# An AdaLN block with a routed feed-forward on one core: last parts of 128 or 64 tokens, and a first chunk in two halves

## The chip, the cores and the metric

The kernel runs on one core of one Trainium2 chip. The metric is the device time of one execution in microseconds (us). The core has a matrix engine (TensorE, PE in the profile), a vector engine (VectorE, DVE), a scalar engine (ScalarE, ACT), a general engine (GpSimd, POOL), a sync engine that issues transfers (SP), and 16 DMA engines. All data are fp32. One fp32 matmul appears in the trace as two records.

## The reference

`x` has 4 sequences of 1024 tokens with 256 features. Six rows of modulation per sequence come from `c`. Then there is a gated linear recurrence and a feed-forward in which each token goes to 2 of 8 experts.

```python
mod = (silu(c) @ wmod).reshape(4, 6, 1, 256)
sa, ca, ga, sb, cb, gb = mod[:, 0], ..., mod[:, 5]      # ga, gb: magnitude at least 0.25
h = layernorm(x) * (1 + ca) + sa
x = x + ga * attn(h)
h = layernorm(x) * (1 + cb) + sb
x = x + gb * ffn(h)

def attn(x):
    xn = rms_scale * x / (rms(x) + EPS) * split_scale
    K = sigmoid(xn @ W_K)
    u, g_in, g_out = split(xn @ W_ugg, 3)
    u = u * sigmoid(g_in) * (1 - K)
    s = scan(s_t = K_(t-1) * s_(t-1) + u_t)
    return (s * sigmoid(g_out)) @ W_out + x

def ffn(x):
    weights, experts = normalised top 2 of softmax(x @ Wg + bg)
    return sum over the two e of weight * (gelu(x @ W1[e] + b1[e]) @ W2[e] + b2[e])
```

## The kernel before

The order of the work on all five engines is the order in which the program writes it (`manual_schedule`). Each engine runs its own list in that order, and semaphores make it wait for the others.

The first part goes through the 4096 tokens in eight chunks of 512 (`c_` from 0). A chunk is normalised and modulated, scaled by its root mean square, turned so that features lie on partitions (`hT`), and multiplied by the four projections `k`, `gi`, `u`, `go`: in `project`, four columns blocks `hc` of 128, each four products of 512 tokens. VectorE does the scan, TensorE the product with `W_out`. In the same loop the gate product `pl` (`f_gate`, L564) runs in four groups of 32 PSUM partitions, and the tokens are entered in one list for each expert.

The first chunk has its own code, since nothing has been prepared for it. It loads `c`, `x` and the modulation matrix `wmod`; `keep_busy(n)` issues n transposes whose result nobody reads; `pt_c` is the transposed silu(c), from which `scT` and `scB` are copied; `pm` (L991) is the modulation of the first sequence on all partitions, and `all_rows` (L290) that of all four. VectorE computes the statistics (a power on POOL between), ScalarE the normalisation, then come the two modulation steps per tile (L996, L999), the squares, the root, and the scale. Eight transposes `pta` (L1014) and two copies (L1015, L1016) make `hT`, and `project(0, 0)` starts with `pk` (L417). `other_rows` and the statistics of chunk 1 follow on VectorE.

The second part goes through the experts' lists in blocks of 256 tokens (`TK`). There can be up to 39 blocks (`NJ`). With two experts for each of 4096 tokens there are at least 32 (`sure`). Which expert a block `j` belongs to and where it starts in the list is computed on the chip: three tables, the last in `late_table`, which is written when block 8 is at work. A block consists of:

- `fetch_used`: the entries of block j+3, and, with two blocks' lead, a gather of the rows `hb` by POOL and the expert's weights by SP;
- `b_up`: the first product `ph` (256 to 1024 features) on the rows turned earlier (`xT`), with gelu on ScalarE;
- `b_turn(j + 1)`: VectorE turns the rows of the next block (L915);
- `b_down`: the second product `pye` (1024 to 256 features, L958) in two parts `t` of 128 tokens; each has its bias added (L972), is multiplied by its weight and gate (L973), and is added to the output by an indirect DMA from POOL (`add_rows`, L945).

The last block of an expert is filled only in part. If it has no more than 128 tokens it is a half block: 128 columns in the first product, one part in the second. In `late_table`, whole blocks and half blocks are counted; all whole ones come first in the order. The number of whole ones (`n_whole`) and of all (`n_blocks`) is loaded into registers, and from block 28 on a branch chooses the code for a whole or a half block (`work_either`). From block 32 on, each further block lies in the branch of the one before (`rest`).

Scatters into the output must not overtake each other, as two blocks can hold the same token. From block 31 on the last part of a block is therefore kept in `last_y`, with its places in `last_at` (L968 copies them), and the scatter is issued at the start of the next block:

```python
def rest(j: int):
    with tc.If(n_blocks > j):
        add_rows(last_y, last_at, T)
        work_either(j, True)
        if j + 1 < NJ:
            rest(j + 1)
```

There is one `last_y`, so it can only be written again when the scatter that reads it has landed.

Of the kernel before, what the change touches and what calls it, by code (L numbers as in the profile page):

```python
# [19 lines left out]
def tile_adaln_block(  # L20
# [33 lines left out]
    nc = tc.nc  # L54
# [92 lines left out]

    nc.sync.dma_start(out=c_sb, in_=c)
    load_x(0, nc.scalar)
    nc.sync.dma_start(out=wmod_sb[:, :, : 2 * D], in_=wmod_r[:, :, : 2 * D])  # L150
    nc.sync.dma_start(out=wmod_sb[:, :, 2 * D :], in_=wmod_r[:, :, 2 * D :])
# [5 lines left out]
    load_x(2, nc.sync)  # L157


    nc.gpsimd.memset(wg_sb, 0.0)  # L160
# [52 lines left out]
    def stats(xb, what: str):  # L213

        st = small.tile([P, TPB, 6], F32, tag="st", name=f"st_{what}")
        mv = small.tile([P, TPB, 2], F32, tag="mv", name=f"mv_{what}", bufs=4)
        rstd = small.tile([P, TPB], F32, tag="rstd", name=f"rstd_{what}", bufs=4)
        for n in range(TPB):
            nc.vector.bn_stats(st[:, n, :], xb[:, n, :])
        for n in range(TPB):  # L220
            nc.vector.bn_aggr(mv[:, n, :], st[:, n, :])
        nc.vector.tensor_scalar_add(rstd, mv[:, :, 1], LN_EPS)  # L222
        nc.gpsimd.tensor_tensor(rstd, rstd, expo[:, 0, :], ALU.pow)  # L223
        return mv, rstd

    def shift(c_):
        mv, rstd = X[c_]["stats"]
        nmr = small.tile([P, TPB], F32, tag="nmr", name=f"nmr_{c_}")
        X[c_]["nmr"] = nmr
        nc.vector.scalar_tensor_tensor(nmr, mv[:, :, 0], -1.0, rstd, ALU.mult, ALU.mult)  # L230

    def norm(dst, c_):
        xb, nmr, (_, rstd) = X[c_]["x"], X[c_]["nmr"], X[c_]["stats"]
        for n in range(TPB):
# [25 lines left out]
    def keep_busy(n: int):  # L260

        for _ in range(n):
            nc.tensor.transpose(idle[:, :P], ident, ident)  # L263

    keep_busy(14)
# [3 lines left out]
    nc.vector.tensor_copy(scT.rearrange("p k b -> p (k b)"), pt[:, : KC * B])  # L269

    scB = setup.tile([P, KC, P], F32, tag="scB", name="scB")
    nc.vector.tensor_copy(scB, scT[:, :, 0:1].broadcast_to((P, KC, P)))
    keep_busy(8)
    mda = deep.tile([P, 2, D], F32, tag="mda", name="mda_0")
# [3 lines left out]
    nc.scalar.dma_start(out=b1_sb, in_=b1.rearrange("e (c p) -> (e c) p", p=P))  # L278
    nc.scalar.dma_start(out=wg_sb[:, :, :E], in_=Wg.rearrange("(k p) e -> p k e", p=P))
    nc.scalar.dma_start(out=bg_sb, in_=bg.rearrange("(o e) -> o e", o=1).broadcast_to((P, E)))  # L280
    X[0]["stats"] = stats(X[0]["x"], "a0")
    shift(0)
    a_norm(0)

    rows_sb = setup.tile([B, 6, D], F32, tag="rows_sb", name="rows_sb")

    def all_rows(i: int):
# [9 lines left out]
        nc.scalar.copy(rows_sb[:, 2 * i : 2 * i + 2, :].rearrange("b r d -> b (r d)"), pm[:B, :])  # L297
# [66 lines left out]
    def a_square(c_):  # L364
        u = work.tile([P, TPB, D], F32, tag="u", name=f"u_{c_}", bufs=1)
        X[c_]["u"] = u
        h = X[c_]["h"]
        ss = small.tile([P, TPB], F32, tag="ss", name=f"ss_{c_}")
        X[c_]["ss"] = ss
        for n in range(TPB):  # L370
# [4 lines left out]
    def a_root(c_):  # L375
        ss = X[c_]["ss"]
        nc.vector.tensor_scalar(ss, ss, 1.0 / D, 1e-30, ALU.mult, ALU.max)
        nc.gpsimd.tensor_tensor(ss, ss, expo[:, 1, :], ALU.pow)

    def a_scale(c_):  # L380
        h, ss, u = X[c_]["h"], X[c_]["ss"], X[c_]["u"]
        nc.vector.tensor_scalar_add(ss, ss, RMS_EPS)
        nc.vector.reciprocal(ss, ss)
        for n in range(TPB):
# [17 lines left out]
    def project(c_, hc, mid=()):  # L402
# [11 lines left out]
        def product(w, col, what):  # L414
            ps = ps_mm.tile([P, TB], F32, tag="mm", name=f"p{what}_{c_}_{hc}")
            for k in range(KC):
                nc.tensor.matmul(  # L417
                    ps,
                    lhsT=w[:, k, col : col + P],
                    rhs=hT[:, k, :],  # L420
# [5 lines left out]
        ps = product(wk_sb, hc * P, "k")  # L426
# [818 lines left out]
```

## Time and profile before

| | |
|---|---|
| median of three runs | 787.91 us (787.7 to 790.15) |
| the profiled execution | 789.1 us |
| its span, first to last instruction | 787.4 us |
| mean granted TensorE clock | 0.997 |
| TensorE busy | 772.8 us, 98% |
| VectorE busy | 504.3 us, 64% |
| GpSimd busy | 290.3 us, 37% |
| ScalarE busy | 241.7 us, 31% |

All times in the profile come from one execution and count from the start of its span. In a line of a timeline the columns are: start, duration, engine, line of the code, operation, tile written and tiles read, shape, count of instructions, and in brackets how long the engine idled before it and what ended that. A line with `x16` stands for sixteen instructions in a row. In the table of stretches each engine's column is its busy time in the stretch and the number of instructions, followed by the granted clock, the busy share of the DMA engines, and GB/s. The chain of waits follows the work back from the last instruction and gives each engine's share of the span.

### The profile page before, as it was taken

What the parts mean: (1) busy time and instruction counts of PE and PEld (TensorE: products, weight loads), DVE (VectorE), ACT (ScalarE), POOL (GpSimd) and SP (SyncE); (2) the same over time, 40 slices, a digit from 0 to 9 for tenths busy, and PEclk for the clock granted to TensorE, in tenths of its full rate; (3) what the DMA queues carried; (4) which work ended last, traced back from release to release, by engine and by line L of the source; (5) the groups of instructions that cost most, each with busy time, mean ns of one, the idle gap of its engine ahead of it and who ended that gap; (6) DMA issues with size and microseconds to landing.
All of it is one profiled execution on the core that took longest, in us unless ns stands there. A gap on an engine that the chain in (4) does not pass through costs nothing.

```text
span 787.4 us, 10804 instructions
## 1 busy us (share of the span) xinstructions
PE 772.8 (98%) x3279; PEld 577.1 (73%) x3279; DVE 504.3 (64%) x1391; ACT 241.7 (31%) x560; POOL 290.3 (37%) x370
## 2 busy tenths in 40 slices
PE   8999999999999999999999999999999999999995
PEld 5455545454546557888888888888888888888994
DVE  5787877898789869767547453544536354453563
ACT  4434243534433343223222122221312222131231
POOL 2102010106142712456564564634434243343431
PEclk9999999999999999999999999999999999999998
DMA  8321334042313265799469898898878687885781
GB/s 296 95 70 47 116 102 142 23 127 86 100 55 113 55 185 183 241 328 258 73 161 206 249 247 253 245 294 223 235 211 230 186 235 217 218 232 167 221 264 25
DMA packets 116040, 138.13 MB, mean 175 GB/s; under 512 B 25782, under 2 KB 100090, under 8 KB 115968
## 3 DMA queue, kind: packets, MB, share of 16 engines
q1 hardware_dynamic: 97184, 111.46, 45.0%
q0 software_dynamic: 17216, 25.25, 15.9%
q10 hardware_dynamic: 1568, 0.57, 0.3%
q8 instruction: 32, 0.52, 0.3%
q14 instruction: 40, 0.33, 0.1%
HBM read 113.52 MB, written 25.42 MB: 176 GB/s over the span
## 4 chain that ended last, share of the span: by engine, by line
PE 83%; DMA 8%; DVE 4%; issue 2%; POOL 1%; ACT 1%; POOLq 0%; DVEq 0%
PE ph_False L928 25%; PE pye_False L958 23%; PE pya L454 7%; PE pk L417 6%; PE pgi L417 6%; PE pu L417 6%; PE pgo L417 6%; DMA hb<-hx,ent 5%; DMA out_dram<-yb_False,ent 2%; PE idle L263 1%; DMA proj<-in_L_ffn_W_dram 1%; PE pm L290 1%; PE pta L399 1%; PE pl L564 1%; DVE s L443 0%
## 5 line engine op out<-in xcount | busy, mean ns | idle before, releaser
L937 ACT ACTIVATE g_False<-ph_False,bb 128x256 f32<-128x256 f32 x248 | 103.8, 470 | 303.0 <-issue 188.2
L915 DVE STREAM_TRANSPOSE xT<-hb 32x128 f32<-32x128 f32 (+1 forms) x576 | 168.8, 293 | 12.7 <-DMA hb<-hx,ent 3.6
L958 PE MATMUL pye_False<-w,g_False 128*128 128x256 f32 x672 | 148.7, 379 | 0.0
L928 PE MATMUL ph_False<-xT,w 128*128 128x256 f32 x672 | 148.6, 379 | 0.0
L928 PEld LDWEIGHTS ph_False<-xT,w 128*128 128x128 f32 x672 | 127.4, 190 | 17.9 <-issue 0.7
L958 PEld LDWEIGHTS pye_False<-w,g_False 128*128 128x128 f32 x672 | 127.5, 190 | 17.6 <-issue 0.2
L945 POOL DMA_INDIRECT out_dram<-yb_False,ent x46 | 73.4, 1595 | 139.9 <-DVE yb_False L973 138.4
L972 DVE TENSOR_TENSOR yb_False<-pye_False,b2b 128x256 f32<-128x256 f32 x42 | 17.8, 424 | 126.3 <-PE pye_False L958 123.8
L586 POOL DMA_INDIRECT lists<-pay,placei x64 | 66.4, 1037 | 38.5 <-DMA ent<-lists 27.4
L928 PE MATMUL ph_False<-xT,proj 128*128 128x256 f32 x320 | 70.8, 379 | 0.7 <-DMA proj<-in_L_ffn_W_dram 0.7
L958 PE MATMUL pye_False<-proj,g_False 128*128 128x256 f32 x320 | 70.7, 379 | 0.0
L928 PEld LDWEIGHTS ph_False<-xT,proj 128*128 128x128 f32 x320 | 60.7, 190 | 9.3 <-DVE yb_False L972 1.0
L958 PEld LDWEIGHTS pye_False<-proj,g_False 128*128 128x128 f32 x320 | 60.8, 190 | 8.3
L830 POOL DMA_INDIRECT hb<-hx,ent x53 | 55.6, 1048 | 22.4 <-issue 15.6
L417 PE MATMUL pk<-hT,proj 128*128 128x512 f32 x128 | 61.0, 599 | 0.7 <-ACT hT L1015 0.7
L223 POOL TENSOR_TENSOR rstd_f<-rstd_f,expo 128x4 f32<-128x4 f32 x8 | 8.2, 1022 | 142.4 <-DVE rstd_f L222 98.8
L417 PE MATMUL pu<-hT,proj 128*128 128x512 f32 x128 | 60.2, 592 | 0.0
L417 PE MATMUL pgo<-hT,proj 128*128 128x512 f32 x128 | 60.2, 592 | 0.0
L417 PE MATMUL pgi<-hT,proj 128*128 128x512 f32 x128 | 60.2, 592 | 0.0
L454 PE MATMUL pya<-wo,z 128*128 128x256 f32 x256 | 56.8, 380 | 0.0
L454 PEld LDWEIGHTS pya<-wo,z 128*128 128x128 f32 x256 | 48.4, 190 | 8.6 <-issue 2.4
L972 DVE TENSOR_TENSOR yb_False<-pye_False,wo_sb 128x256 f32<-128x256 f32 x20 | 8.5, 424 | 60.4 <-PE pye_False L958 60.3
(234 smaller groups left out, 811.1 us busy)
## 6 DMA issues: line engine op xcount, KB each, us to landing
w<-in_L_ffn_W_dram SPq DMA_DIRECT2D x48, 1024.0 KB
proj<-in_L_ffn_W_dram SPq DMA_DIRECT2D x24, 1024.0 KB
hx<-gb SPq DMA_DIRECT2D x4, 1024.0 KB
out_dram<-x SPq DMA_DIRECT2D x8, 512.0 KB
hx<-h SPq DMA_DIRECT2D x8, 512.0 KB
x<-in_L_attn_x_dram SPq DMA_DIRECT2D x7, 512.0 KB
swapped<-u SPq DMA_DIRECT2D x7, 512.0 KB
hT<-swapped SPq DMA_DIRECT2D x28, 128.0 KB
```

What stands on the lines that cost most here:

```text
L223: nc.gpsimd.tensor_tensor(rstd, rstd, expo[:, 0, :], ALU.pow)
L263: nc.tensor.transpose(idle[:, :P], ident, ident)
L417: nc.tensor.matmul(ps, lhsT=w[:, k, col : col + P], rhs=hT[:, k, :], start=(k == 0), stop=(k == KC - 1),)
L454: nc.tensor.matmul(py[:, t, :], lhsT=z[hc][:, ts(2 * q + t, P)], rhs=wo[:, hc, :], start=(hc == 0), stop=(hc == HC - 1),)
L586: ins = nc.gpsimd.indirect_dma_start(out=lists[:, :], out_offset=IndirectOffsetOnAxis(ap=place, axis=0), in_=what, in_offset=None, bounds_ ...
L830: nc.gpsimd.indirect_dma_start(out=hb[:, t, :], out_offset=None, in_=hx[: seen(j), :], in_offset=IndirectOffsetOnAxis(ap=BK[j]["ent"][:, t ...
L915: nc.vector.transpose(to[ts(q, SQ), :, :, ts(i, SQ)], hb[ts(i, SQ), :, :, ts(q, SQ)])
L928: nc.tensor.matmul(ph[:, u, :], lhsT=w1[:, k, ts(fc, P)], rhs=xT[:, k, :n], start=(k == 0), stop=(k == KC - 1),)
L937: nc.scalar.activation(g[:, fc, :n], ph[:, u, :], AF.Gelu_apprx_tanh, bias=bb[:, fc : fc + 1])
L945: return nc.gpsimd.indirect_dma_start(out=out_rows[:n], out_offset=IndirectOffsetOnAxis(ap=at, axis=0), in_=yb, in_offset=None, bounds_che ...
L958: nc.tensor.matmul(py, lhsT=g[:, fc, ts(t, P)], rhs=w2[:, fc, :], start=(fc == 0), stop=(fc == FC - 1),)
L972: nc.vector.tensor_add(yb, py, b2b)
```

## The change

In the second part, a block can now have 256, 192, 128 or 64 tokens (`sizes`). The first product has 256 columns for the first two and 128 for the last two, as before. The last part of the second product has 128 or 64 tokens, chosen by a branch that stands around this part alone. A part of 64 tokens writes its eight products alternately to partitions 0 to 63 and 64 to 127 of the PSUM tile, and VectorE adds both halves. `late_table` counts four kinds of blocks, so its tables have 32 columns instead of 16, and four numbers are loaded into registers instead of two. Branches begin at block 26 instead of 28.

In the first chunk, `x` is loaded in two halves of 256 tokens on two queues; statistics, normalisation, squares, root, scale, turn, and the four products of `hc` 0 are done by halves. The loads of `b1`, `Wg` and `bg` move from ScalarE's queue to SP's, behind the `x` of chunk 2. `keep_busy` issues fp32 matmuls on zeros instead of transposes, 12 and 5 of them instead of 14, 8 and 18. The copies of `scT` and `scB` move from VectorE to ScalarE, and those of the `all_rows` results go behind the scale of the second half. `first_turn(1)`, `other_rows` and the statistics of chunk 1 come between the products of the two halves.

```diff
...
     nc.sync.dma_start(out=c_sb, in_=c)
-    load_x(0, nc.scalar)
+    nc.scalar.dma_start(out=X[0]["x"][:, halves[0]], in_=x0[:, halves[0]])
     nc.sync.dma_start(out=wmod_sb[:, :, : 2 * D], in_=wmod_r[:, :, : 2 * D])
+    nc.sync.dma_start(out=X[0]["x"][:, halves[1]], in_=x0[:, halves[1]])
...
     load_x(2, nc.sync)
+    nc.sync.dma_start(out=b1_sb, in_=b1.rearrange("e (c p) -> (e c) p", p=P))
     nc.gpsimd.memset(wg_sb, 0.0)
+    nc.sync.dma_start(out=wg_sb[:, :, :E], in_=Wg.rearrange("(k p) e -> p k e", p=P))
+    nc.sync.dma_start(out=bg_sb, in_=bg.rearrange("(o e) -> o e", o=1).broadcast_to((P, E)))
...
         for _ in range(n):
-            nc.tensor.transpose(idle[:, :P], ident, ident)
-
-    keep_busy(14)
+            nc.tensor.matmul(idle[:, :P], lhsT=zero, rhs=zero, start=True, stop=True)
+
+    keep_busy(12)
...
-    nc.vector.tensor_copy(scB, scT[:, :, 0:1].broadcast_to((P, KC, P)))
-    keep_busy(8)
...
+    nc.scalar.copy(scB, scT[:, :, 0:1].broadcast_to((P, KC, P)))
+    keep_busy(5)
...
+    for at in halves:
+        stats_of(X[0]["x"], tiles0, at)
+        shift(0, at)
+        norm(X[0]["h"], 0, at)
...
+            half, done = TB // 2, {}
+            for what in args:
+                if what == "go":
+                    halved()
+                done[what] = product(*args[what], what, slice(0, half))
+
+            def out_of(what):
+                return product(*args[what], what, slice(half, TB), done[what])
...
+    QT = P // 2
+    sizes = [TK, TK - QT, P, QT]
+    NS = len(sizes)
...
-        whole = blocks_of(float(P - 1), "lw")
-        some = blocks_of(float(TK - 1), "ls")
...
+        upto = [
+            blocks_of(float(TK - 1 - (sizes[k + 1] if k + 1 < NS else 0)), f"l{k}")
+            for k in range(NS)
+        ]
...
+    def down_part(j: int, t: int, n: int = P, mid=None, keep: bool = False):
+
+        g, w2, b2b, ent, hb = (BK[j][k] for k in ("g", "w2", "b2b", "ent", "hb"))
+        py = ps_y.tile([P, D], F32, tag="y", name=f"pye_{j}_{t}_{n}")
+
+        beside = P // n
+        for fc in range(FC):
+            nc.tensor.matmul(
+                py[ts(fc % beside, n), :],
+                lhsT=g[:, fc, ds(t * P, n)],
+                rhs=w2[:, fc, :],
+                start=(fc < beside),
+                stop=(fc >= FC - beside),
+            )
...
+        nc.vector.tensor_add(yb[:n], py[:n], b2b[:n])
+        if beside > 1:
+            nc.vector.tensor_add(yb[:n], yb[:n], py[n:])
...
-    for n in range(TPB):
+
+    def first_mod(n: int):
...
+    for n in range(HT):
+        first_mod(n)
+    a_square(0, halves[0])
+    a_root(0, halves[0])
     nc.vector.tensor_mul(rs_sb, rms_sb, split_sb)
-    for i in range(6 * D // TB):
+    first_mod(HT)
+    a_scale(0, halves[0])
+    for n in range(HT + 1, TPB):
+        first_mod(n)
+    a_square(0, halves[1])
+    for i in range(6 * D // TB - 1):
         all_rows(i)
-    keep_busy(18)
-    a_scale(0)
...
+    first_turn(0)
+    all_rows(6 * D // TB - 1)
+    a_root(0, halves[1])
+    nc.scalar.copy(mda[:, 0, :], pm[:, :D])
+    nc.vector.tensor_scalar_add(mda[:, 1, :], pm[:, D:], 1.0)
+    a_scale(0, halves[1])
+    all_rows_copied()
...
+        project(
+            c_, 0, [lambda: a_norm(nxt)] if more else [],
+            None if c_ else lambda: (
+                first_turn(1), other_rows(), load_mdf(0), a_stats(1), shift(1)
+            ),
+        )
...
+        def large():
+            first(False)
+            down_part(j, 0)
+            either(
+                j, 0, lambda: down_part(j, 1, keep=keep), lambda: down_part(j, 1, QT, keep=keep)
+            )
+
+        def small_():
+            first(True)
+            either(
+                j, 2, lambda: down_part(j, 0, keep=keep), lambda: down_part(j, 0, QT, keep=keep)
+            )
+
+        either(j, 1, large, small_)
...
```

`first` issues `fetch_used`, `b_up` and `b_turn(j + 1)`. `either(j, k, larger, smaller)` builds only `larger` where block j must, on any routing, be among the first kinds up to k, only `smaller` where it cannot be, and otherwise both in a branch on the register `n_upto[k]`.

## The prediction

> **What bounds the kernel now.** I read the page first, then the busy time by stretches, then the timelines of the last 45 us and of the first 25 us, because the diff touches only these two ends and one table in the middle. The page:
>
> ```profile
> span 787.4 us, 10804 instructions
> PE 772.8 (98%) x3279; PEld 577.1 (73%) x3279; DVE 504.3 (64%) x1391; ACT 241.7 (31%) x560; POOL 290.3 (37%) x370
> PE 83%; DMA 8%; DVE 4%; issue 2%; POOL 1%; ACT 1%; POOLq 0%; DVEq 0%
> ```
>
> TensorE is busy 98% of the span, so a saving must take matmul time away or fill the 14.6 us in which it idles. The stretches tell where (columns: length, then busy time and count of each engine):
>
> ```profile
> 429.00:700.00 271.00, 271.00 (x1258) 238.51 (x1257) 131.24 (x408) 65.40 (x156) 118.22 (x122) 1.00 0.83 235
> 742.00:778.00 36.00, 35.60 (x242) 32.85 (x240) 24.46 (x96) 11.40 (x40) 11.12 (x8) 1.00 0.71 206
> ```
>
> In the whole blocks nothing but TensorE counts. In the tail its idle time is also small (0.4 us), but the timelines show that a second chain runs just beside it:
>
> ```profile
> 735.16 7.07 PE L958 MATMUL pye_False<-w,g_False 128*128 128x256 f32 x32
> 742.07 3.73 PE L928 MATMUL ph_True<-xT,w 128*128 128x128 f32 x32
> 763.30 3.81 PE L928 MATMUL ph_True<-xT,w 128*128 128x128 f32 x32
> 770.41 3.73 PE L928 MATMUL ph_True<-xT,proj 128*128 128x128 f32 x32
> 773.98 3.62 PE L958 MATMUL pye_True<-proj,g_True 128*128 128x256 f32 x16
> ```
>
> ```profile
> 759.21 4.00 DVE L915 STREAM_TRANSPOSE xT<-hb 32x64 f32<-32x64 f32 x16 [1.00 <-DMA hb<-hx,ent]
> 764.55 0.15 DVE L968 COPY last_at<-ent 128x1 int32<-128x1 int32 x1 [1.35 <-DMA out_dram<-last_y,last_at]
> 765.64 4.00 DVE L915 STREAM_TRANSPOSE xT<-hb 32x64 f32<-32x64 f32 x16
> 770.16 0.15 DVE L968 COPY last_at<-ent 128x1 int32<-128x1 int32 x1 [0.52 <-DMA out_dram<-last_y,last_at]
> 777.63 0.42 DVE L972 TENSOR_TENSOR last_y<-pye_True,wo_sb 128x256 f32<-128x256 f32 x1 [1.82 <-PE pye_True L958]
> ```
>
> ```profile
> 771.83 1.56 POOL L945 DMA_INDIRECT out_dram<-last_y,last_at  x1 [4.37 <-DVE last_y L973]
> 778.93 1.56 POOL L945 DMA_INDIRECT out_dram<-last_y,last_at  x1 [5.55 <-DVEq L1203]
> ```
>
> The reader should see that L968 waits for the previous scatter to land before `last_y` may be overwritten, that VectorE turns the next block's rows for 4.0 us, and that block 34's first product (763.30) starts when its turn ends (763.21), not when TensorE is free.
>
> **The tail.** From the router on these inputs the experts get 1849, 1836, 484, 383, 1127, 837, 1258 and 418 tokens. Cut in 256s, the remainders are 57, 44, 228, 127, 103, 69, 234 and 162. Before, that is 31 whole and 5 half blocks, as the trace has it. After, 30 whole, one of 192 (j=30), three of 128 (31 to 33) and two of 64 (34, 35). The first product is not changed. A second-product part is 16 records of 0.216 us, 3.45 us. The part of 64 tokens has the same 16 records, put alternately in the two halves of PSUM's partitions; it is shorter only if two of them run side by side. The nearest row is the gate product, which uses four groups of 32 columns:
>
> ```profile
> 95.88 0.65 PE L564 MATMUL pl<-hT,wg_sb 128*32 128x128 f32 x16
> ```
>
> Sixteen records of 128 columns at 0.108 us (half of the 256-column 0.216) would take 1.73 us one after another; they took 0.65. So groups do overlap, here 2.7-fold for four. [...]
>
> [...] Each 64-token part has one more VectorE add (0.42 us, the row of L972, because the halves are summed). I carry the timeline forward, each step with its own duration of before:
> - Block 30: the second part ends at 740.35 instead of 742.07; three VectorE steps (0.42+0.42+0.48) instead of two; the scatter goes out at 742.25 instead of 743.50.
> - Block 31: b_up from 740.35, down to 747.4; its scatter 749.45 (750.73 before). Its landing took 6.4 us, so L968 goes at 755.85 (757.15), scatter 32 at 757.15, and lands 6.1 us later (as before) at 763.25.
> - hb(34) is gathered 1.9 us behind that scatter, at 751.3, lands 6.5 us later at 757.8, is turned by 761.9: b_up(34) at 761.95 instead of 763.30. Its 64-token down ends at 767.4.
> - Block 35: VectorE first waits for that landing, does block 33's steps (1.1), then turns 4.0 to 768.35: b_up(35) at 768.4 instead of 770.41, although TensorE was free at 767.4. Down ends at 773.9 instead of 777.6.
> - Block 34's `last_y` comes after that turn: scatter 770.7 instead of 771.83; it lands 3.8 us later at 774.5; block 35's four steps (0.15+0.42+0.42+0.48) and the 0.58 to issue give the last scatter at 776.55 instead of 778.93.
>
> So 2.4 us of the 5.2 arrive at the end. Bounds: -1.0 if the gather of 34 lands no earlier (the 16 DMA engines are full with weights from 752 to 769), -3.5 if landings are as short as the shortest, 3.7 us. The weights of 35 landed at 768.9 and are needed at 772.1, so they cover. What lies behind the last scatter (8.4 us: landing and the closing barrier) is kept.
>
> Branches: 10 blocks (j from 26) instead of 8 are branched, each with a second branch between its two products, and four registers are loaded instead of two (0.3 to 0.5 us each at 697). On TensorE a compare-and-branch took 0.07 to 0.22 us, twice more (0.445 at 738.46, 3.70 at 775.37), and it is fetched 2 to 3 us ahead of the array, so I cost them at nothing. VectorE has about 0.5 us at each, hidden in its waits for scatters (0.5 to 2.7 us idle). Price without that cover: 0.2 us for each of 10 on TensorE, 2 us. [...] I use the ordinary rows, because before's five half blocks already jump over a whole variant and only one jump was long.
>
> **The table.** `late_table` runs 429.59 to 435.05 on VectorE. Two more `blocks_of` (0.6 each), two more differences and starts (0.6), and four operations on 736 instead of 368 elements (0.54 to about 0.93, 1.56 in all), two more folds (0.8): +4.2 us. Behind it wait block 8's `yb` steps, its scatters on POOL and the gather of block 11. Their next need is at 452 to 453, and VectorE idles half of that stretch (131 of 271 us), so I cost it at nothing; if block 11's rows come late, up to 4 us.
>
> **The front.**
>
> ```profile
> 4.69 0.37 PE L268 MATMUL pt_c<-ident,sc 4*128 4x4 f32 x2
> 6.75 2.25 PE L991 MATMUL pm<-wmod_sb,scB 128*128 128x512 f32 x4
> 14.18 2.19 PE L263 MATMUL idle<-ident 128*128 128x128 f32 x18
> 17.91 1.98 PE L417 MATMUL pk<-hT,proj 128*128 128x512 f32 x4 [0.67 <-ACT hT L1015]
> ```
>
> TensorE waits here for VectorE and ScalarE. The keep-busy products become true fp32 ones, two records each: 24 records ahead of pt_c instead of 14. At 0.21 us each (the cold row: 14 took 3.25) that is 5.1 us from about 1.05, and pt_c slips from 4.69 to 6.2, with the scT and scB copies, pm and the first `first_mod` behind it: pm ready at 10.0 instead of 9.0. [...] Against this, x arrives in halves, so statistics, mods, root and scale of half 0 are done before half 1's; the four products of half 0 start (256 columns, 0.86 us each) while half 1 is finished. I get pk at 16.65 instead of 17.91, and project(0,0) done at 24.0 instead of 25.05. The small loads moved from ScalarE's queue pass to SP's, behind x2 and ahead of x3: three issues of about 0.5 us there, not needed before 90 us. The 18 fillers go; the gaps of 1.5 to 2 us that they leave lie after 8 us of dense matmuls. Then `other_rows` and the statistics of chunk 1 come some 2.5 us later on VectorE, so nu·pu and go wait and hold PSUM buffers: about 0.4 us of TensorE waits come back. Net -0.9 us; bounds -2.0 (warm early) and +0.5 (cold, with a longer VectorE line).
>
> Sum: -2.4 + 0 + 0 - 0.9 = -3.3 us. The profiled execution took 789.1 (span 787.4), so it would be 785.8 (784.1). That one stands 1.2 above the median of the runs, 787.91; from the median, 784.6.
>
> **The rivals.**
> - *The whole TensorE saving arrives*: scatters land faster than in the trace, the tail gives 5.2 and the front 0.9: 781.8. For it: TensorE has 98%. Against: the rows of L968 and of xT above.
> - *The two ends give nothing*: the column halves do not overlap, or the chain alone sets the tail, and the front's slip of pt_c eats its gain: 787.5 to 788. Here the change doesn't do what it says. For it: 24 cold records ahead of pt_c. Against: the pl row.
> - *Slower: code fetch at the branches*. Ten blocks get a jump between the two products where before there was straight code. If such a jump stalls for the 3.7 us of the long record, less the 2 us lead, five or more misses of 1.7 us cost 8.5 against 3.3: 793. It decides from the second miss (2 x 1.7 = 3.4) on. For it: the 0.445 and the 3.70. Against: all ordinary jumps.
>
> **How the numbers follow.** Likeliest case (chain-limited tail, small front gain) 50%, 783.0 to 786.4; whole saving 17%; nothing 16%; slower 17%. About 0.3% (2.4 us) is what a measurement of this kernel can tell from no change, so faster means below 785.5. The likeliest case lies below that by four fifths: 0.40 + 0.17, with a little from the nothing case, 0.58 faster; 0.25 same; 0.17 slower. The range reaches from 781.5 to 789.5.
>
> **What would show it.** Right: second parts of j = 30, 34 and 35 in 1.7 to 1.8 us; block 35's first product about 2 us after block 34's last matmul has ended or less, waiting for xT; the last scatter 2 to 3 us nearer. Front: pk at 16 to 17. Wrong: 64-token parts of 3.4 us; TensorE idle with only branches ahead of it; pk later than 17.9; idle TensorE near 452 to 460; a lower granted clock in the first slices.

## The result, and the profile after

The changed kernel takes 795.34 us in the median of six runs (794.11 to 801.89), the kernel before beside it 788.41 (787.7 to 790.46). The ratio is 1.0098, with a 95% interval of 1.0077 to 1.0118: 6 to 9 us slower, where 3.3 us faster was forecast. The profiled execution took 795.39 us (span 793.7).

The same three lines of the page as the prediction shows, now of the changed kernel (called "after" from here on):

```profile
span 793.7 us, 11029 instructions
PE 769.4 (97%) x3289; PEld 573.7 (72%) x3289; DVE 509.6 (64%) x1412; ACT 242.4 (31%) x563; POOL 290.4 (37%) x373
PE 43%; DMA 27%; issue 14%; POOL 7%; DVE 5%; ACT 1%; POOLq 1%; another core or an unknown queue 0%; SPq 0%; DVEq 0%
```

TensorE's busy time fell by 3.4 us on balance, and the timeline below shows the shorter parts. But it idles 24.3 us of the span instead of 14.6, and its share of the chain that ended last went from 83% to 43%. The waits of TensorE in after (columns: who waited for what, us in total, times, longest) name the new ones:

```profile
PE ph_False L996 <- DMA w<-in_L_ffn_W_dram: 3.2, 1, 3.2
PE ph_True L996 <- DVE yb L1044: 1.9, 1, 1.9
PE ph_True L996 <- DVE xT L983: 1.7, 1, 1.7
PE ph_True L996 <- issue: 1.5, 1, 1.5
PE ph_False L996 <- DVE yb L1041: 1.1, 2, 0.6
```

All five stand ahead of a block's first product (L996). TensorE's timeline of after places them:

```profile
455.06 7.14 PE L996 MATMUL ph_False<-xT,w 128*128 128x256 f32 x32 [3.25 <-DMA w<-in_L_ffn_W_dram]
...
718.33 7.17 PE L996 MATMUL ph_False<-xT,proj 128*128 128x256 f32 x32 [0.57 <-DVE yb L1041]
...
732.98 7.17 PE L996 MATMUL ph_False<-xT,w 128*128 128x256 f32 x32 [0.57 <-DVE yb L1041]
739.99 5.49 PE L1028 MATMUL pye<-w,g 128*128 128x256 f32 x32
747.42 3.81 PE L996 MATMUL ph_True<-xT,w 128*128 128x128 f32 x32 [1.93 <-DVE yb L1044]
...
770.45 3.81 PE L996 MATMUL ph_True<-xT,w 128*128 128x128 f32 x32 [1.55 <-issue]
774.19 2.01 PE L1028 MATMUL pye<-w,g 128*64 128x256 f32 x16
777.87 3.84 PE L996 MATMUL ph_True<-xT,proj 128*128 128x128 f32 x32 [1.67 <-DVE xT L983]
781.64 2.01 PE L1028 MATMUL pye<-proj,g 128*64 128x256 f32 x16
```

The reader sees the shorter parts (7.07 became 5.49, 3.62 became 2.01) and, around them, idle stretches that add up to more than they saved. Start times in both executions, and what lies between:

| | before | after | difference |
|---|---|---|---|
| `project(0, 1)` starts | 24.89 | 24.19 | -0.70 |
| block 9, first product | 438.18 | 437.84 | -0.34 |
| block 12 (past the late weights of block 10) | 479.62 | 482.76 | +3.14 |
| block 30 (past two waits of 0.57) | 728.26 | 732.98 | +4.72 |
| block 31 (one part of 64, then 1.93 idle) | 742.07 | 747.42 | +5.35 |
| block 33 | 756.12 | 761.55 | +5.43 |
| block 34 (turn of rows late) | 763.30 | 770.45 | +7.15 |
| block 35 (part of 64, turn late) | 770.41 | 777.87 | +7.46 |
| last scatter | 778.93 | 785.43 | +6.50 |

Ahead of block 34 the profile names no cause ("issue"), but VectorE's turn of its rows ends at 770.36, 0.09 us before the product:

```profile
766.36 4.00 DVE L983 STREAM_TRANSPOSE xT<-hb 32x64 f32<-32x64 f32 x16 [0.72 <-DMA hb<-hx,ent]
```

The table is of one execution of each kernel. It leaves four questions: the late weights of block 10, behind the longer `late_table` (+3.5), the waits of 0.57 (+1.6), the stall ahead of block 31 (2.2 from start to start, after a part that saved 1.7), and the tail.

### The profile page after: what moved, and what is told of

The parts are those of the page before. It is cut to its first block, busy times and chain, and to the rows that moved or that the text cites. A ratio compares the mean times of both kernels' runs of the same rounds, so it can differ in the third digit from the quotient of the medians.

```text
span 793.7 us, 11029 instructions
## 1 busy us (share of the span) xinstructions
PE 769.4 (97%) x3289; PEld 573.7 (72%) x3289; DVE 509.6 (64%) x1412; ACT 242.4 (31%) x563; POOL 290.4 (37%) x373
## 4 chain that ended last, share of the span: by engine, by line
PE 43%; DMA 27%; issue 14%; POOL 7%; DVE 5%; ACT 1%; POOLq 1%; another core or an unknown queue 0%; SPq 0%; DVEq 0%
DMA out_dram<-yb,ent 13%; DMA hb<-hx,ent 8%; PE pya L505 7%; PE pk L449 6%; PE pgi L449 6%; PE pgo L449 6%; PE pu L449 6%; PE ph_False L996 5%; POOL out_dram L1014 5%; PE pye L1028 4%; DMA lists<-pay,placei 4%; DMA ent<-lists 3%; PE idle L286 1%; POOL lists L638 1%; PE pta L430 1%
## 5 line engine op out<-in xcount | busy, mean ns | idle before, releaser
L1005 ACT ACTIVATE g<-ph_False,bb 128x256 f32<-128x256 f32 x248 | 104.0, 471 | 308.0 <-issue 158.2
L1028 PE MATMUL pye<-w,g 128*128 128x256 f32 (+1 forms) x720 | 156.5, 380 | 0.4 <-DMA w<-in_L_ffn_W_dram 0.4
L996 PE MATMUL ph_False<-xT,w 128*128 128x256 f32 x672 | 148.8, 380 | 3.8 <-DMA w<-in_L_ffn_W_dram 3.2
L1028 PEld LDWEIGHTS pye<-w,g 128*128 128x128 f32 (+1 forms) x720 | 132.6, 188 | 20.1 <-issue 1.5
L996 PEld LDWEIGHTS ph_False<-xT,w 128*128 128x128 f32 x672 | 127.3, 190 | 22.4 <-issue 4.3
L1014 POOL DMA_INDIRECT out_dram<-yb,ent x46 | 73.2, 1592 | 146.6 <-DVE yb L1044 145.0
L1028 PE MATMUL pye<-proj,g 128*128 128x256 f32 (+1 forms) x352 | 76.3, 379 | 0.0
L1028 PEld LDWEIGHTS pye<-proj,g 128*128 128x128 f32 (+1 forms) x352 | 64.9, 188 | 9.1
L996 PE MATMUL ph_False<-xT,proj 128*128 128x256 f32 x320 | 70.9, 380 | 0.6 <-DVE yb L1041 0.6
L996 PEld LDWEIGHTS ph_False<-xT,proj 128*128 128x128 f32 x320 | 60.6, 190 | 9.3 <-DVE yb L1041 1.0
L449 PE MATMUL pk<-hT,proj 128*128 128x512 f32 (+1 forms) x132 | 61.2, 585 | 0.2 <-ACT rows_sb L327 0.2
L449 PE MATMUL pgo<-hT,proj 128*128 128x512 f32 (+1 forms) x132 | 60.4, 580 | 0.0
L449 PE MATMUL pu<-hT,proj 128*128 128x512 f32 (+1 forms) x132 | 60.3, 579 | 0.0
L449 PE MATMUL pgi<-hT,proj 128*128 128x512 f32 (+1 forms) x132 | 60.3, 579 | 0.0
```

The costliest lines, as they stand in the source:

```text
L449: nc.tensor.matmul(ps[:, at], lhsT=w[:, k, col : col + P], rhs=hT[:, k, at], start=(k == 0), stop=(k == KC - 1),)
L996: nc.tensor.matmul(ph[:, u, :], lhsT=w1[:, k, ts(fc, P)], rhs=xT[:, k, :n], start=(k == 0), stop=(k == KC - 1),)
L1005: nc.scalar.activation(g[:, fc, :n], ph[:, u, :], AF.Gelu_apprx_tanh, bias=bb[:, fc : fc + 1])
L1014: return nc.gpsimd.indirect_dma_start(out=out_rows[:n], out_offset=IndirectOffsetOnAxis(ap=at, axis=0), in_=yb, in_offset=None, bounds_che ...
L1028: nc.tensor.matmul(py[ts(fc % beside, n), :], lhsT=g[:, fc, ds(t * P, n)], rhs=w2[:, fc, :], start=(fc < beside), stop=(fc >= FC - beside),)
```

## The experiments

Ratios are to runs of the kernel before on the same chip, with 95% intervals; 0.1% is 0.8 us. Where two kernels are compared by their ratios and ran on different chips, the text gives both figures or a range. A trace is one execution, and what it shows need not be in the others. In the diffs, lines with + are new.

**The first chunk alone.** e1 is before with the hunks of the first chunk and none of the blocks.

> The kernel before with the first-chunk part of the change alone; blocks, table and branches as before. Theory: this part gives what the trace of after shows at block 8 and no more, TensorE 0.34 us earlier at 438 us, so 0.3 to 0.7 us faster than before, and the 6.5 us that after lost are all in the other part. Rival: part of the loss comes from the front (chunk 1's statistics later, small loads later), then this kernel is 1 us or more slower than before.

Measured: 1.0012 (1.0002 to 1.0023), about 1 us slower. At block 8 TensorE waits for weights in its trace, for 2.19 us where the trace of before has 0.67:

```profile
425.97 8.83 PE L980 MATMUL ph_False<-xT,proj 128*128 128x256 f32 x32 [2.19 <-DMA proj<-in_L_ffn_W_dram]
```

The 32 records took 8.83 us instead of 7.07. The stretches of the same kernel show why (the figure after the engines is the granted clock):

```profile
428.00:430.00 2.00, 2.00 (x6) 1.55 (x5) 1.87 (x8) 0.84 (x2) 1.69 (x2) 0.50 1.12 72
```

After 2.19 us of idle the clock stood at half for some 3.5 us (the two stretches around this one, 426 to 428 and 430 to 432, have 0.70 and 0.95). The stall cost its 2.19 us and 1.76 more. That is more than the kernel loses in its median: the traced execution took 793.0 us, the median of 14 is 790.58. So the place is shown, the usual size is not.

**A slower table in before.** e2:

```diff
             tab["l"], ends_at = late_table()
+            spare = wo_sb.rearrange("p c d -> p (c d)")[:, D:]
+            for _ in range(4):
+                nc.vector.tensor_add(spare, spare, spare)
+            nc.vector.tensor_add(spare[:, :D], spare[:, :D], spare[:, :D])
```

> The kernel before with five idle additions (4.3 us of VectorE, results unused) right behind late_table in block 8; nothing else. Theory: the longer table alone makes block 10's weights late, through block 8's scatters, the list scatter behind them on GpSimd, and the load of a block's entries that stands ahead of the weights on SP's queue; TensorE idles about 3 us ahead of block 10's first product, and the kernel is 3 us slower than before. Rival: the idle time at 455 us in after comes from other traffic, and VectorE's slack hides 4 us here as I had forecast: no idle time, same as before within 0.5 us.

Measured: 1.0043 (1.0025 to 1.0061), 2 to 5 us slower, by nothing but VectorE work that I had called hidden. Its trace has the wait in the same place, block 10's first product; before's trace, shown first, has none there:

```profile
451.99 7.07 PE L928 MATMUL ph_False<-xT,w 128*128 128x256 f32 x32
```

```profile
452.80 7.14 PE L928 MATMUL ph_False<-xT,w 128*128 128x256 f32 x32 [1.65 <-DMA w<-in_L_ffn_W_dram]
```

The way is seen on the queues of GpSimd (first line) and SP. Before:

```profile
438.17 1.03 POOL L586 DMA_INDIRECT lists<-pay,placei  x1 [0.19 <-issue]
443.10 0.37 SPq L822 DMA_DIRECT2D ent<-lists  x1
444.15 0.25 SPq L852 DMA_DIRECT2D w<-in_L_ffn_W_dram  x1
```

After:

```profile
442.50 1.03 POOL L638 DMA_INDIRECT lists<-pay,placei  x1 [0.19 <-issue]
445.83 0.37 SPq L890 DMA_DIRECT2D ent<-lists  x1
446.76 0.37 SPq L920 DMA_DIRECT2D w<-in_L_ffn_W_dram  x1
```

Block 10's weights were issued 7.84 us ahead of their use in before (452.0). In after they were used 8.30 us after their issue, as soon as they were there, so before can have had little room to spare. They are issued 2.61 us later in after, because the load of a block's entries stands ahead of them on SP's queue. That load waits for a list scatter on POOL (4.33 us later), and this stands behind block 8's scatter into the output (440.59 instead of 436.26), which waits for VectorE, which is at the table.

**The table in block 11.** e3 is after with the table moved:

```diff
-        elif j == NE:
+        elif j == NE + 3:
             tab["l"], ends_at = late_table()
```

> The kernel after with late_table written in block 11 instead of block 8 (it is needed from block 14 on); its size is unchanged. Theory: from block 10 on the weights are fetched a block earlier, so the cover is there, the 3.25 us of idle TensorE ahead of block 10 vanish, and the kernel is 3.0 to 3.3 us faster than after. Rival: another wait of a block's weights takes its place in block 13 or 14, and it gains under 1 us.

The wait for block 10's weights is gone from the trace. The time is 1.0070 (1.0045 to 1.0095), against 1.0098 and, in a second measurement (e5), 1.0078 for after. So only 0.6 to 2.2 us reach the end, where 3.0 to 3.3 were expected, and the intervals overlap: no gain is shown. In the traced execution what was won was partly lost later: 2.48 us idle ahead of block 31 (1.93 in after), and 3.18 us ahead of block 35 (1.67), followed by a clock of 0.50.

**The small variant first.** e4 is after with the two variants of a block exchanged in the code:

```diff
+            if k == 1:
+                with tc.If(n_upto[k] < j + 1) as it_is:
+                    smaller()
+                with it_is.Else():
+                    larger()
+                return
```

> The kernel after with the two variants of a block exchanged in the code: the one with 128 columns in the first product stands ahead of the one with 256. Theory: TensorE's 2.97 us compare-and-branch at 743.9 is a fetch of code, because the jump from the end of block 30's large variant over its small one and block 31's large one is the longest in the kernel; with the order exchanged no jump there is that long, the record falls under 0.5 us, block 31's first product starts 2 us earlier, and the kernel is 1 to 2 us faster than after. Rival 1: TensorE waited there for VectorE (the profile names yb L1044), which stays, so no change. Rival 2: the miss moves to another block, for instance at the first large block or the end, and costs as much.

Measured: 1.0036 (1.0021 to 1.0051), 3 to 5 us less than after, more than expected. TensorE's compare-and-branch instructions in before, after and e4 (columns: engine queue, count, shortest/median/longest in ns, first and last start):

```profile
L1153 PEldq COMPARE_BRANCH  x11: 65/185/445, 697.8 to 768.5; - x11
```

```profile
L1252 PEldq COMPARE_BRANCH  x25: 65/179/2967, 684.2 to 779.6; - x25
```

```profile
L1258 PEldq COMPARE_BRANCH  x18: 65/178/331, 685.5 to 777.6; - x18
```

The record of 2967 ns in after starts at 743.91 and ends 0.5 us before block 31's first product. The page had put this wait down to `yb`; e4 leaves VectorE's work as it is, and block 31 starts without idle time. The way there passes block 30's small variant and block 31's large one, 72 matmuls of code; in before the same way passed 56, and its branch took 445 ns. With the small variant first nothing that long is passed.

What the branch waited for is seen on the DMA queue q8, which the page calls an instruction queue. In the whole blocks of before and after it carries one packet of 16 KB for each 255 or so instructions of TensorE, matmuls and weight loads almost all of them (237 to 272 between two packets), so it brings TensorE's code. Between 743.9 and 746.9 it has one packet (columns: packets, MB, share of 16 engines), from 744.57 to 745.53:

```profile
q8 instruction: 1, 0.02, 2.0%
```

The four other records of 3.2 to 3.5 us (e3, e5, e13b, e14b) have one each, begun 0.7 us after the record's start and ended 1.1 to 1.4 us before its end. Ahead of block 10, where the weights were late, there is none. So I take the wait ahead of block 31 for a fetch of code. The record took 3.0 to 3.5 us in these five traces, of which 1.9 to 2.6 us showed as idle time in four.

What e4 won is more than this stall's 2 us, and the rest was not isolated. Its trace also has 0.37 us instead of 1.55 ahead of block 34, and the exchange moves all code behind it.

**The changed kernel again**, beside the next three:

> The changed kernel itself, beside the next three on one chip. Theory: 6 to 8 us slower than before, as in the first comparison; the trace shows again the late weights of block 10, two waits of about 0.57 us ahead of the first products of blocks 29 and 30, and one compare-and-branch of about 3 us ahead of block 31. Rival: one or more of these were chance of one execution, then they are missing here and the time is 2 us or more nearer to before.

Measured: 1.0078 (1.0051 to 1.0105). All waits are there again, but their sizes differ: block 10 waited 0.61 us in this execution, block 31 2.30 and then ran at a clock of 0.50 (5.31 us instead of 3.73), block 35 3.04 and again at half clock (5.47). It is the slowest of six (798.4 us, median 796.62). The kinds of waits are the kernel's, their sizes are one execution's.

**Three repairs together**: e6 is after with the late table, the small variant first, and at the end of each small variant

```diff
+            for _ in range(2):
+                nc.vector.memset(spare, 0.0)
```

> The kernel after with late_table in block 11, the small variant ahead of the large one in the code, and two one-column memsets on VectorE at the end of each small variant, which bring the two variants to nearly the same count of VectorE instructions. Theory: the small variant was filled up to the large one's semaphore count at its turn of rows, so that TensorE's first product in the next block waited for a count that a large block reaches only at its last add; with equal counts the two waits of 0.57 us vanish. All three repairs together: 3 + 2 + 1.5 us less than after, 0 to 1 us slower than before, and the late turns of blocks 34 and 35 remain. Rival: the waits of 0.57 us are for VectorE's data (the last part's sum), then they stay and the gain is 5 us or less.

Measured: 1.0008 (0.9992 to 1.0024), the same as before; 5.5 us less than after on one chip. The waits of 0.57 us are gone. In after, block 30's first product (732.98) begins as VectorE's first add for block 29's second part ends (732.94), a result that it doesn't read. My explanation, which no trace shows: the small variant of these blocks has three VectorE instructions fewer than the large one since the extra add came in (two before); its turn of rows is counted up to make good, and TensorE, which waits for that turn, then waits in a large block for the first add of the last part. That the memsets, which add two instructions to the small variant, remove the waits agrees with it.

But in e6's trace TensorE also stops for 1.70 us inside block 33's first product, after 21 of its 32 records, and for 2.60 us inside block 34's, after 14. No branch and no wait stands there. In both stretches q8 has a packet (756.9 to 759.6, and 766 to 768.6):

```profile
q8 instruction: 1, 0.02, 2.4%
```

```profile
q8 instruction: 1, 0.02, 2.2%
```

So exchanging the variants took away the one long branch, but code still came late elsewhere.

e13b has the memsets alone:

> The kernel after with only the third repair: two one-column memsets on VectorE at the end of each small variant. Theory: the first products of blocks 29 and 30 no longer wait for the last add of the block before, the two idle stretches of 0.57 us (0.75 us from start to start) vanish, and it is 1 to 1.5 us faster than after; the fetch of about 3 us ahead of block 31 and the late weights stay, so 4.5 to 6 us slower than before. Rival: whatever is won there is lost again in the tail, which the weights set, and the gain is under 0.5 us.

Measured: 1.0085 (1.0068 to 1.0103), no gain to be seen. Both waits are absent from its trace, and block 31 waits 2.57 us for the fetch, longer than in after: the rival in size. Whether the gain was lost in the tail, as the rival says, one trace does not tell.

**The three repairs with the first chunk as before:**

> The same three repairs, with the first chunk as before. Theory: the first-chunk part brings nothing at the end, since its 0.7 us are lost again at block 8, which waits for its weights; so within 0.5 us of the kernel with the three repairs. Rival: the front's part of the change costs about 1 us, then this one is 1 us faster; or it brings 0.7 us, then it is as much slower.

Measured: 0.9982 (0.9970 to 0.9994), 2 us less than e6. In its trace block 33 waits 0.31 us for code instead of 1.70, block 34 not at all, and block 35 waits 1.69 us for its turn.

**The gather first.** e8 is e6 with two `last_y`, and in the blocks from 32 on

```diff
             fetch_used(j, half)
+            if j >= sure_any:
+                add_rows(last_ys[(j - 1) % 2], last_ats[(j - 1) % 2], T)
             b_up(j, half)
```

instead of `add_rows` ahead of `work`.

> The kernel with the three repairs, and two changes in the blocks from 32 on: last_y and last_at exist twice, so that a block's last sum needn't wait for the previous scatter to land, and the gather of block j+2 is issued ahead of the scatter of block j-1. Theory: what holds the last two blocks back is the gather that stands behind the scatter and lands late among the weights, so their turns come 1.5 to 2 us earlier, TensorE's idle time ahead of blocks 34 and 35 (1.5 and 1.7 us in after) nearly vanishes, and the kernel is 2 to 3 us faster than the one with the three repairs, and 1 to 2 us faster than before. Rival: the scatters must land one after another in any case, each now issued 1.5 us later, so the end moves by less than 0.5 us or gets later.

Measured: 0.9962 (0.9948 to 0.9977), 3 us faster than before and 3.6 less than e6. Not all of this need be the gather's: the 4.3 us for which code kept TensorE waiting in e6's trace are missing too (at the same record of block 33, e8 is 0.15 us late). From block 9 to the end TensorE has no idle stretch of 0.3 us, and block 35 follows block 34 at once:

```profile
766.60 2.01 PE L1030 MATMUL pye<-w,g 128*64 128x256 f32 x16
768.76 3.84 PE L996 MATMUL ph_True<-xT,proj 128*128 128x128 f32 x32
772.53 2.01 PE L1030 MATMUL pye<-proj,g 128*64 128x256 f32 x16
```

The same without the changed first chunk, e9:

> The kernel with the three repairs, two last_y and the gather ahead of the scatter, and the first chunk as before. Theory: the first-chunk part costs 1 to 2 us at the end, so this is 1 to 2 us faster than the same kernel with that part (3 us faster than before), 4 to 5 us faster than before. Rival: the time of the front is hidden here, and it is the same as with it, 3 us faster than before.

Measured: 0.9983 (0.9972 to 0.9995), less gain than e8, and none against e7 (0.9982). Its TensorE is 1.9 us earlier at block 31 than e8's and loses that in block 33, ahead of the second product:

```profile
759.67 3.69 PE L978 MATMUL pye<-w,g 128*128 128x256 f32 x16 [1.97 <-issue]
```

The weights are the first suspect, because the DMA engines are full in the stretch ahead of it (last two columns: busy share of the DMA engines, GB/s):

```profile
753.90:760.00 6.10, 4.13 (x35) 3.95 (x35) 4.90 (x21) 2.29 (x8) 2.58 (x2) 1.00 1.08 330
```

They are not the cause. This block's weights were issued at 737.97 and 739.86, 20 us earlier, and had landed by 747.84. Between 757.0 and 759.7 the queue q8 has a packet again, from 757.14 to 758.11:

```profile
q8 instruction: 1, 0.02, 2.2%
```

The same holds for every kernel with the three repairs. In those with the first chunk as before, code is late at block 33's second product: 0.31 us in e7, 1.97 in e9, 1.52 in e10 and 0.78 in e16b. In those with the changed first chunk, which has 10 matmul records and 10 weight loads more, it is late 11 matmul records earlier, inside the first product: 1.70 us in e6, 0.15 in e8 and 0.51 in e15b. TensorE goes on 1.4 to 1.6 us after the packet has ended wherever it waits 0.3 us or more. The border between two packets of code, which moves by the instructions added ahead of it, fits this; what makes the wait long or short was not found.

As an estimate, a half block's 2 MB of weights need 6.4 us at 330 GB/s, and on TensorE it takes 7.03 us (754.52 to 761.55 in after), or 5.3 with a part of 64. So the weights would be next, but in no trace with the three repairs does TensorE wait for them after block 10.

Both of these on one chip, once more:

> The kernel of e8 (three repairs, two last_y, gather ahead of the scatter, the changed first chunk), beside the same kernel with the first chunk as before, on one chip. Theory: the tail waits for the weights of block 33 at a time that the first chunk does not move, so both have the same time within 0.7 us, 2 to 3 us faster than before. Rival: the first-chunk part has its own price near block 8, as e6 and e7 suggest, then this one is 1 us or more slower than its partner.

> The kernel of e9 (three repairs, two last_y, gather first, the first chunk as before), beside the same kernel with the changed first chunk, on one chip. Theory: the same time as its partner within 0.7 us. Rival 1: 1 us or more faster. Rival 2: 1 us or more slower, as the comparison of e8 and e9 across two chips had it; then the first-chunk part does bring its gain to the end.

Measured: 0.9962 (0.9949 to 0.9976) with the changed first chunk, 0.9977 (0.9960 to 0.9995) without. The order is that of e8 and e9, but the intervals overlap. So a gain from the changed first chunk is not shown; what it seems to bring here (1.2 to 1.6 us) is of the size of the code waits above.

**The parts of 64 as parts of 128.** Both variants of a last part get 128 columns, in e9's kernel and in after:

```diff
-                j, 0, lambda: down_part(j, 1, keep=keep), lambda: down_part(j, 1, QT, keep=keep)
+                j, 0, lambda: down_part(j, 1, keep=keep), lambda: down_part(j, 1, keep=keep)
...
-                j, 2, lambda: down_part(j, 0, keep=keep), lambda: down_part(j, 0, QT, keep=keep)
+                j, 2, lambda: down_part(j, 0, keep=keep), lambda: down_part(j, 0, keep=keep)
```

> The same kernel as e9, with both variants of each last part computed with 128 columns: the branches, the tables and the order stay, only the parts of 64 tokens take 3.45 us of TensorE again and lose their extra add. Theory: with the chain of gathers and scatters moved out of the way the parts of 64 tokens bring most of their 3 x 1.7 us, so this one is 3 to 4.5 us slower than e9. Rival: the chain still sets the tail, and the parts bring under 1.5 us.

Measured: 1.0008 (1.0000 to 1.0016), slower than e9 by 2.0 us in the ratios and 2.5 in the medians. So the parts bring about half of their TensorE time here, with a wait for code in block 33 in both traces (1.97 and 1.52 us).

> The kernel after with both variants of each last part computed with 128 columns: branches, tables and order stay, the parts of 64 tokens take 3.45 us of TensorE again and lose their extra add. Theory: in after these parts bring the end little, because the weights and the gathers of the last blocks arrive when they arrive; and without the extra add the waits of 0.57 us go too. So the time is within 1.5 us of after. Rival: the parts bring their 5.2 us of TensorE time less one add, then this kernel is 3 us or more slower than after.

Measured: 1.0043 (1.0027 to 1.0060): 3 to 4 us *faster* than after, which neither theory had. So in the kernel as changed, the parts of 64 with their extra add cost more than they save. Its branch still has the long record, 3233 ns at 738.91, but no idle time over 0.3 us follows:

```profile
735.52 7.07 PE L1028 MATMUL pye<-w,g 128*128 128x256 f32 x32
742.68 3.81 PE L996 MATMUL ph_True<-xT,w 128*128 128x128 f32 x32
```

The sequencer was at this branch at 738.9, and the matmuls of block 30 lasted until 742.6, 3.7 us; in after they ended at 745.5, 1.6 us behind the branch. The full part covers the fetch, and the part of 64 uncovers it. The waits of 0.57 us are gone too.

**Two single pieces in before.** e11 has the gather first and two `last_y` (with the scratch of the table in `wo_sb`, for space):

> The kernel before with two last_y and the gather of block j+2 ahead of the scatter of block j-1, from block 32 on; its table's scratch lies in the place of after, everything else as before. Theory: TensorE set the tail there (0.4 us idle), so it gains under 0.7 us by itself: the chain matters only once the parts get shorter. Rival: the gain of e8 over the three repairs (about 4 us) is the chain's alone and would have come without parts of 64, then 2 us or more.

Measured: 0.9994 (0.9987 to 1.0001), no effect shown: without the parts of 64 TensorE sets the tail, and in this trace its timeline has no wait from block 31 (740.81) to the end of the last product (776.11). e12 has the small loads on SP's queue:

> The kernel before, with the loads of b1, Wg and bg on SP's queue behind the x of chunk 2 (as in after), all else as before. Theory: what the front's part costs near block 8 comes with these loads, so TensorE idles 1 us or more ahead of block 8's first product and the kernel is 0.5 to 1 us slower than before. Rival: it comes with the halves or the order of VectorE, then this kernel is the same as before within 0.3 us.

Measured: 1.0005 (0.9993 to 1.0016), no effect shown, and no wait at block 8 in its trace. So what the first chunk's part costs there was not seen to come with these loads.

## Why the prediction was wrong, point by point

Two terms of the sum were put at 0, the table and the branches, and the change brought a third wait that was not in the sum. With these three repaired (e6) the kernel is level with before, 5.5 us better than after. From there to the forecast the tail (-2.4) and the front (-0.9) are missing.

- *The table costs nothing.* This step failed. The term was named with its 4.2 us (block 8's `yb` went from 435.05 to 439.38, 4.3), and its cover was looked for at the rows of block 11 and in VectorE's idle half. (The 131 us of the row are its busy time; idle are 140 of 271.) SP's queue was not followed: the load of entries stands behind the list scatters, and block 10's weights stand behind it, with a lead of 7.84 us. It cost 3.25 us of TensorE in the profiled execution, 0.61 in another; in before, 4.3 us of VectorE there cost 2 to 5 (e2).
- *Branches cost nothing.* This step failed. The ordinary rows were taken for all jumps; but before's jumps pass at most 56 matmuls, and the change makes the longest 72. Its branch then took 3.0 to 3.5 us in all five traces with the change's branches in their order, with one packet on q8 inside. The rival named the mechanism, but looked for it at the new jumps between the two products; it came at a jump between blocks that was there before. It asked for two misses at 1.7 us; there was one, at 1.9 to 2.6. The price given, the long record less a lead of 2 us, was about right. Missed was that the part of 64 shortens that lead where the jump is taken (3.7 us in e14b, 1.6 in after).
- *The change adds no other wait.* The meeting of two variants was not looked at. With the extra add in one variant TensorE waits in the next block for the last part's add: 0.57 us twice. Alone it did not show in the time (e13b).
- *The parts of 64 save 5.2 us of TensorE.* The sum rests on 1.73 us for such a part, which no run of before shows: the nearest row, the gate product, has four groups that overlap 2.7-fold. It was nearly right: in after TensorE's 16 records take 2.01 instead of 3.62 us with the last one's end, so 1.6 us a part and 4.8 for three. The records start in pairs, 0.21 us from pair to pair.
- *2.4 us of the 5.2 arrive at the end.* In after nothing arrives. The step that failed is the carrying forward with before's landing times. The scatter at 755.95 landed after 8.6 us instead of 6.4, and hb(34), gathered behind it at 757.84, after 8.5 instead of 6.6. Block 34's turn began at 766.36, and its first product was 1.7 us later against block 33's than in before. The two weight loads of block 34 (755.81 and 757.03) went out beside that scatter, the first now just ahead of it where in before both were behind (751.26 and 752.35 against 750.73); that this made the landings longer is likely and not shown. The bound "if the gather of 34 lands no earlier" should have gone on to "lands later". That e10 against e9 gives 2.0 to 2.5 us, near the forecast 2.4, is luck: the chain of scatters that the 2.4 came from is out of the way there, and code is late in both. (One slip in the working: block 31's scatter, carried like the others, comes out at 749.0, not 749.45; it does not bear on the result.)
- *The front brings 0.9 us.* At the start it is about right: pk at 16.74 (16.65 forecast), the next project at 24.19 (24.0), 0.7 us earlier than in before. The bound of -2.0 (warm early) rests on a term that no run shows: in after the 24 records from 1.12 us took 5.48 us, ten more at 6.75 took 1.38, and pm was done at 9.85 (10.0 forecast). Between chunk 1 and block 9 half of it goes. Alone the change of the first chunk is 1 us slower (e1), and 2 us slower in e6 against e7, but not slower in e15b against e16b. Two things stand behind it in the traces, a longer wait at block 8 in some (0.67 us in before, 2.19 in e1, 1.41 in e8, none in after) and the shift of the borders between packets of code; how much each is worth is open.

Open: in all ten traces with the changed first chunk a load of entries some 20 us before block 8 is issued 4.1 to 4.8 us after the list scatter ahead of it, in the eight others 3.0 to 3.6 us (398.46 to 401.58 before, 398.61 to 402.74 in e1). The small loads alone do not bring it (e12: 3.2). What delays it was not found. Nor do the items of one execution give the median: a stall of 2 to 3 us is followed by half the clock in some executions and not in others (0.50 after 2.19 us in e1, 1.00 after 2.57 us in e13b), and code waits differ between executions of one kernel (0.15 us in e8, 0.51 in e15b, at the same record).

The best kernel of these runs is e8, measured again as e15b: three repairs, the gather first, the changed first chunk, 0.9962 both times.

## What to carry to other kernels

Follow a longer step through every queue that waits for it, SP's last of all: the weights behind one small load, issued 2.61 us later, were the path. A shorter piece of work also shortens the cover of whatever the sequencer does behind it, so ask what was hidden under exactly the time that is taken away (3.7 us of matmuls behind the branch in e14b, 1.6 in after). Look at the instruction queue beside every stall that the profile calls "issue", before giving it to weights or data: reordering the code took one long branch away here, and code was late at other places (by 1.70 and 2.60 us in e6, 1.97 in e9). And keep the instruction counts equal where two variants meet: two memsets took away two waits of 0.57 us, in the traces of e6 and e13b.

## What the runs showed of the hardware that I had not expected

- Idle stretches of TensorE of 2.0 to 3.2 us were followed by a granted clock of 0.50 for about 3.5 us in several executions (after 2.19 us in e1, 2.37 in e4, 2.30 and 3.04 in e5, 3.18 in e3, 2.00 in e14b), at a price of 1.5 to 1.8 us; in others of the same length (3.25 in after, 2.60 in e6, 2.57 in e13b, 2.48 in e3) the clock stayed at 1.00.
- One compare-and-branch of TensorE took 2967 to 3533 ns wherever its way passed 72 matmuls of code (after, e3, e5, e13b, e14b), with a packet of 16 KB on q8 inside, and none took more than 638 ns in the kernels that had the small variant first.
- TensorE also waited for code where no branch stood, after 21 of 32 records of a product (1.70 us in e6, 0.51 in e15b) and at a product's first record (1.97 us in e9), and went on 1.4 to 1.6 us after the packet had ended.
